# Scattered additions in pairs, a finer reload of x, and a reordered begin of the first attention in a six-layer kernel

## The chip, the cores and the metric

The kernel runs on one core of a Trainium2 chip. The metric is the device time of one execution in microseconds (us). A core has a matrix engine (PE, with its weight loads PEld), a vector engine (DVE), a scalar engine (ACT), a general engine (POOL), and SP, which here only issues transfers. Each engine works through its own instruction list in order; transfers run beside them on 16 DMA engines. In the profile a line such as L526 is that line of the kernel's file, and "q" behind an engine's name (SPq, POOLq) is its sequencer.

## What is computed

Six residual layers work on `x`, 4096 rows of 256 floats: an expert layer, an attention, the same expert layer again, then a second kind of expert layer, a second attention, and that expert layer again. The change touches the first three and the begin of the fourth. Cut to what matters:

```python
def _L0_ffn_ref(x, Wg, W1, b1, W2, b2):      # E = 8 experts, each takes k = 1024 of the 4096 rows
    S = jax.nn.sigmoid(xt @ Wg).T
    G, I = jax.lax.top_k(S, k)               # an expert's own k rows are all different
    ex = xt[I]
    hid = gelu(einsum('ekh,ehf->ekf', ex, W1) + b1)
    out = (einsum('ekf,efh->ekh', hid, W2) + b2) * G[..., None]
    return zeros_like(xt).at[I.reshape(-1)].add(out.reshape(-1, h))

x = x + 0.5 * _L0_ffn_ref(_layernorm(x), ...)
x = x + _L0_attn_ref(_layernorm(x), ...)     # q, k, v each rotated (rope), 16 heads of 16, causal
x = x + 0.5 * _L0_ffn_ref(_layernorm(x), ...)
x = x + 0.5 * _L1_ffn_ref(_layernorm(x), ...)
x = x + _L1_attn_ref(_layernorm(x), ...)
x = x + 0.5 * _L1_ffn_ref(_layernorm(x), ...)
```

## The kernel before

`x` lies on the chip as 32 tiles of 128 rows; four tiles are one sequence (a "group", QT = 4). PE, DVE, ACT and POOL run in program order in the layers of interest (`manual_schedule`); SP's order is chosen by a scheduler from what is ready.

**Expert layer (`_ffn0`, L246).** It runs twice (n = 0 and 1). A gate (`Gate`, L1285) comes first. In layer 0 it is the loop at L276 over eight groups g: for even g the moments of the next two groups (`moments`, L1312: bn_stats L175 and bn_aggr L176 for each tile on DVE, one square root on ACT L181, five small DVE operations L210 to L215), then `columns` (L1336: PE transposes, ACT copies L1343), `rows` of the next group (L1326: normalises four tiles, tiles 1 and 3 on POOL, the others on DVE), `thin` (L1345: scores with `wg`, ACT copy `line` L1353) and `tall` of the group before (L1355: PE transposes the scores, ACT copies them into `raw` at L1362). `sigmoid` (L1364) then clips at -87, takes exp on ACT, adds 1, takes the reciprocal. A search for each expert's 1024th score follows (L321), and `indices` (L430) makes the row lists.

Then come eight experts (L539). For each: `gather` (L471, eight indirect transfers issued by POOL), `turn` (transposes), `hidden` (64 matmuls of 512 columns on each half, PE and ACT), `outputs` (L512). `outputs` makes eight tiles `ob` of 128 rows; each is added into `acc_d` in memory by one indirect transfer with addition (L526), issued by POOL, and each waits until the one before it has landed. In layer 0 `clear` (L149) writes zeros into the buffers of a later layer, two transfers for each expert, issued by SP before `hidden`. After the last expert SP reloads `x` from `acc_d` in four pieces of eight tiles (L558).

**First attention (`_attn0`, L566).** It loads its weights on SP (L578 to L594), POOL writes its constants (L597 to L631), DVE makes `mask_h` and `ident_h` (L610, L612). The begin (L849 to L882) takes the moments of tiles 0 to 7 (`ln_range`, with the square root on ACT), prepares the bias `bo` with a small matmul (L855), then handles sequence 0: `normal` (L641: xn on DVE, and POOL adds `bo` to the residual rows, L653), `turned` (transposes), `rope` (L662) for k, q and v. One rope half copies the product to `raw` (ACT, L671), then POOL makes the cosine and the sine product (L673, L675), and for the second half POOL combines them (L680, L681). `sides` (L697) projects and SP copies the heads into `wide` tiles (L714). The moments of the other tiles stand between. `top` (L739) makes scores on PE and DVE takes the row maxima (L759). From there a loop of 16 pairs of steps runs; the gate of the next expert layer is spread over its last part as `units` (L1371).

**Second kind of expert layer (`ffn1_before`, L1784).** It begins with the moments of tiles 0 to 7 (L1794), `normal` of groups 0 and 1, `columns`, and then logits, a routing and POOL's sends.

`ln_guess` (L184) is a second way to 1/sqrt, with twelve small DVE operations and none on ACT.

Of the kernel before, what the change touches and what calls it, by code (L numbers as in the profile page):

```python
# [9 lines left out]
F32 = mybir.dt.float32  # L10
# [9 lines left out]
P = 128  # L20
# [45 lines left out]
class Kernel:  # L66
    def __init__(self, ctx, tc, w):
# [7 lines left out]
        self.late = self.wide = None  # L75


        self.x = resid.tile([P, TT, D], F32, name="x")
        x_in = w["x"].rearrange("(t p) d -> p t d", p=P)
        for g in range(TT // QT):  # L80
# [68 lines left out]
    def clear(self, zero, part, parts):  # L149

        for t in PARTS:
            rows = self.slots_d[t].rearrange("(j p) d -> p j d", p=P)
            a, b = slot_tiles(t) * part // parts, slot_tiles(t) * (part + 1) // parts
            self.nc.sync.dma_start(out=rows[:, a:b, :], in_=bc(zero, 1, b - a))


    def ln_tiles(self, pool):
# [88 lines left out]
    def _ffn0(self, ctx, n, front):  # L246
# [253 lines left out]
        def hidden(e, h, w1, beside=lambda: None):  # L500
            hid[h] = work.tile([P, FC, CH], F32, name="hid")
            for f in range(FC):
# [6 lines left out]
                nc.scalar.activation(hid[h][:, f, :], hp, AF.Gelu, bias=b1[:, e, f : f + 1])  # L509
                beside()  # L510

        def outputs(e, h, w2, following=None):  # L512
            for i in range(QT):
                if i % 2 == 1 and following is not None:
                    turn(following, i // 2)
                st = h * QT + i
                op = psum.tile([P, D], F32, name="op", tag="o")
                for f in range(FC):
                    nc.tensor.matmul(  # L519
                        op, lhsT=hid[h][:, f, i * P : i * P + P], rhs=w2[:, f, :],  # L520
                        start=(f == 0), stop=(f == FC - 1),
                    )
                ob = work.tile([P, D], F32, name="ob", bufs=4)
                nc.vector.tensor_tensor(ob, op, b2[:, e, :], ALU.add)  # L524
                nc.scalar.mul(ob, ob, gate[:, e, st : st + 1])  # L525
                nc.gpsimd.indirect_dma_start(  # L526
                    out=acc_d[:, :],
                    out_offset=bass.IndirectOffsetOnAxis(ap=idx[:, e, st : st + 1], axis=0),
                    in_=ob, in_offset=None,
                    bounds_check=NT - 1, oob_is_err=True, compute_op=ALU.add,  # L530
                )

        if n == 0:
            zero = pool.tile([P, D], F32, name="zero")
# [4 lines left out]
        for e in range(E0):  # L539
            w1, w2 = wts  # L540
            if e + 1 < E0:
                wts = weights(e + 1)
            coming = indices(e + 1) if e + 1 < E0 else iter(())
            if n == 0:
                self.clear(zero, e, E0)

            hidden(e, 0, w1, lambda: advance(coming, 1))
            advance(coming, 99)
            if e + 1 < E0:
                gather(e + 1)  # L550
            if e == 0:
                turn(0, 1)
            outputs(e, 0, w2)
            hidden(e, 1, w1)
            outputs(e, 1, w2, e + 1 if e + 1 < E0 else None)
        for g in range(4):
            ts = slice(g * 8, g * 8 + 8)
            nc.sync.dma_start(out=self.x[:, ts, :], in_=acc_rows[:, ts, :])  # L558


    def attn0(self, front):
# [4 lines left out]
    def _attn0(self, ctx, front):  # L566
# [43 lines left out]
        nc.vector.tensor_copy(mask_h, maskT)  # L610
        ident_h = pool.tile([P, P], BF16, name="ident_h")
        nc.vector.tensor_copy(ident_h, self.ident)  # L612

        tops = []
        for i in range(4):
# [21 lines left out]
        def bank(shape, name):  # L637
            return psum.tile(shape, F32, name=name, tag="m", bufs=2)


        def normal(b):  # L641
            mv, rstd = stats
            st = seq[b] = {}
            xn = st["xn"] = work.tile([P, QT, D], F32, name="xn", bufs=1)
            st["xnT"] = work.tile([P, DC, CH], F32, name="xnT", bufs=1)
            for i in range(QT):
                t = b * QT + i
                nc.vector.tensor_scalar(
                    xn[:, i, :], self.x[:, t, :], mv[:, t, 0:1], rstd[:, t : t + 1],
                    ALU.subtract, ALU.mult,  # L650
                )
            rows = self.x[:, b * QT : b * QT + QT, :]
            nc.gpsimd.tensor_tensor(rows, rows, bc(bo, 1, QT), ALU.add)  # L653

# [7 lines left out]
        def rope(b, n, c):  # L662
            st = seq[b]
            pp = bank([P, CH], "pp")
            for k in range(DC):
                nc.tensor.matmul(
                    pp, lhsT=first[n][:, k, c * P : c * P + P], rhs=st["xnT"][:, k, :],
                    start=(k == 0), stop=(k == DC - 1),
                )
            raw = work.tile([P, CH], F32, name="raw")  # L670
            nc.scalar.copy(raw, pp)  # L671
            xc = work.tile([P, CH], F32, name=f"xc{c}", bufs=1)
            nc.gpsimd.tensor_tensor(xc, raw, cos, ALU.mult)  # L673
            xs = work.tile([P, CH], F32, name=f"xs{c}", bufs=1)
            nc.gpsimd.tensor_tensor(xs, raw, sin, ALU.mult)  # L675
            st["half", c] = (xc, xs)
            if c == 1:
                r = st["rope", n] = work.tile([P, DC, CH], F32, name=f"rope{n}", bufs=1)
                (ec, es), (oc, os_) = st["half", 0], st["half", 1]
                nc.gpsimd.tensor_tensor(r[:, 0, :], ec, os_, ALU.add)  # L680
                nc.gpsimd.tensor_tensor(r[:, 1, :], oc, es, ALU.subtract)  # L681
# [169 lines left out]
        bvw = work.tile([P, CH], F32, name="xs0", bufs=1)[:, : DC * P].rearrange("p (c o) -> p c o", c=DC)  # L851
# [6 lines left out]
        normal(0)  # L858
        for c in range(DC):
            turned(0, c)  # L860
        for n in (1, 0):
            for c in range(DC):
                rope(0, n, c)
        self.ln_range(pool, stats, 8, 8)
        for c in range(DC):
            rope(0, 2, c)
# [418 lines left out]
class Gate:  # L1285


    def __init__(self, k, n, ctx):
        self.k, nc = k, k.nc
        self.pool = pool = ctx.enter_context(k.tc.tile_pool(name=f"g0_{n}", bufs=1, reuse_waits="tile"))  # L1290
        self.xn_d = k.dram.tile([NT, D + E0], F32, name=f"xn_d{n}")
        self.acc_d = k.dram.tile([NT, D], F32, name=f"acc_d{n}")
        self.xn_rows = self.xn_d.rearrange("(t p) d -> p t d", p=P)
        self.acc_rows = self.acc_d.rearrange("(t p) d -> p t d", p=P)
        self.wg = pool.tile([P, DC, E0], F32, name="wg")
        nc.sync.dma_start(out=self.wg, in_=k.w["Wg"].rearrange("(c p) e -> p c e", p=P))
# [58 lines left out]
    def tall(self, g, bank):  # L1355
        nc = self.k.nc
        tp = bank()[:, : QT * E0]
        for i in range(QT):
            nc.tensor.transpose(
                tp[:, i * E0 : i * E0 + E0], self.line[g][:, i * P : i * P + P], self.k.ident[:E0, :E0]  # L1360
            )
        nc.scalar.copy(self.raw[:, g * QT : g * QT + QT, :].rearrange("p t e -> p (t e)"), tp)  # L1362

    def sigmoid(self, t0, t1):  # L1364
        nc, r = self.k.nc, self.raw[:, t0:t1, :]
        nc.vector.tensor_scalar(r, r, -87.0, None, ALU.max)
# [417 lines left out]
def ffn1_before(k, f):  # L1784
# [3 lines left out]
    with ExitStack() as ctx, k.tc.manual_schedule(engines={E.PE, E.DVE, E.Activation, E.Pool, E.SP}):  # L1788
# [305 lines left out]
```

## Time and profile before

| what | us |
|---|---|
| runs before | 3935.51, 3939.59, 3947.90 (median 3939.59) |
| the profiled execution | 3937.4 |
| its span | 3935.6 |
| PE busy | 3603.7 (92% of the span) |
| DVE / ACT / POOL busy | 1870.9 / 1451.8 / 1206.7 |
| gate, search and first indices of layer 0 | 0 to 98 |
| experts, layer 0: first `hp` to last `op` | 111 to 574 |
| first attention, from the reload to the next gate's end | 582 to 1252 |
| experts, layer 2 | 1308 to 1771 |

In a line of the page's groups or of the timeline stand start and length in us, the engine, the line, the operation, output and inputs by name, shapes, a count, and in brackets how long the engine had been idle and what ended that. PEclk is the clock that PE was granted. The profile shows one execution; the median of the runs is 2.2 us above it.

### The profile page before, as it was taken

How to read it: one execution, taken by the hardware profiler on the slowest of the kernel's cores; microseconds unless marked ns; L12 is line 12 of the kernel's file. 1: busy time of each engine (PE TensorE's matmuls, PEld its weight loads, DVE VectorE, ACT ScalarE, POOL GpSimd, SP SyncE). 2: the span in 40 equal slices, each digit the busy share in tenths (PEclk: the TensorE clock that was granted, in tenths of full speed). 3: DMA queues.
4: the chain of work that ended last, by engine and by line, in shares of the span. 5: the costliest groups of instructions: out<-in, count | busy, mean ns of one | idle time of the engine just before them, and what ended most of it. 6: DMA issues, size and time to landing. Idle time of an engine off the chain costs nothing.

```text
span 3935.6 us, 51751 instructions
## 1 busy us (share of the span) xinstructions
PE 3603.7 (92%) x18250; PEld 2258.1 (57%) x18250; DVE 1870.9 (48%) x4435; ACT 1451.8 (37%) x2936; POOL 1206.7 (31%) x1072
## 2 busy tenths in 40 slices
PE   4999987999996799996899999999999999989978
PEld 1566653555553466664588745555555554568855
DVE  7221216555554312206534566666555576554444
ACT  3222222444444222221133355555555554523311
POOL 2333334343331333332553312220000005404364
PEclk7999997999988899997999999999999999989989
DMA  9433321100113233324367401000000001146643
GB/s 323 135 77 71 72 45 56 25 19 23 28 33 93 55 70 72 74 30 145 102 217 229 138 20 30 28 22 1 1 1 1 1 1 59 49 122 221 181 146 105
DMA packets 256268, 306.97 MB, mean 78 GB/s; under 512 B 34448, under 2 KB 226064, under 8 KB 255760
## 3 DMA queue, kind: packets, MB, share of 16 engines
q1 hardware_dynamic: 206864, 202.43, 16.4%
q0 software_dynamic: 49152, 101.24, 10.9%
q8 instruction: 151, 2.47, 0.3%
q14 instruction: 101, 0.83, 0.1%
HBM read 161.48 MB, written 133.69 MB: 75 GB/s over the span
## 4 chain that ended last, share of the span: by engine, by line
PE 76%; issue 6%; DVE 6%; DMA 5%; POOL 4%; ACT 3%; POOLq 0%; SPq 0%; DVEq 0%; ACTq 0%
PE hp L505 10%; PE op L519 10%; PE sp L1051 6%; PE tp L1071 6%; PE zp L1098 6%; PE pq L1029 6%; PE hs L1713 4%; PE yp L1113 3%; PE pv L1018 3%; PE yps L1735 2%; PE st L795 2%; PE z L809 2%; PE hp L1640 2%; POOL slots_d L1426 2%; PE sp L750 2%
## 5 line engine op out<-in xcount | busy, mean ns | idle before, releaser
L505 PE MATMUL hp<-exT,w 128*128 128x512 f32 x1024 | 456.0, 599 | 0.0
L519 PE MATMUL op<-w,hid 128*128 128x256 f32 x2048 | 451.9, 379 | 0.0
L1060 ACT ACTIVATE ex<-sp,nmax 128x512 f32<-128x512 f32 x512 | 344.7, 685 | 242.2 <-DVE nmax L1057 242.2
L1533 POOL DMA_INDIRECT yg<-ys_d,slot x256 | 267.1, 1044 | 513.2 <-DVE x L1546 296.5
L519 PEld LDWEIGHTS op<-w,hid 128*128 128x128 f32 x2048 | 387.0, 190 | 63.9 <-issue 14.3
L524 DVE TENSOR_TENSOR ob<-op,b 128x256 f32<-128x256 f32 x128 | 54.3, 424 | 642.9 <-PE op L519 567.5
L526 POOL DMA_INDIRECT acc_d<-ob,idx x128 | 210.8, 1646 | 442.4 <-ACT ob L525 204.5
L1057 DVE TENSOR_REDUCE nmax<-sp 128x2 f32<-128x1024 f32 x256 | 301.5, 1219 | 80.4 <-PE sp L1051 80.2
L759 DVE CUSTOM_DVE_ANT_0 junk<-sp,mask 128x128 bf16<-128x128 f32 (+3 forms) x512 | 251.0, 490 | 183.9 <-PE sp L750 159.7
L505 PEld LDWEIGHTS hp<-exT,w 128*128 128x128 f32 x1024 | 193.9, 192 | 222.3 <-issue 217.6
L1071 PEld LDWEIGHTS tp<-ident,ex 128*128 128x128 f32 x2048 | 234.3, 141 | 146.8 <-issue 85.2
L1713 PE MATMUL hs<-w_sb,xT 128*128 x1264 | 308.7, 388 | 2.3 <-DMA xs<-slots_d 1.3
L509 ACT ACTIVATE hid<-hp,b 128x512 f32<-128x512 f32 x256 | 175.9, 687 | 323.9 <-PE hp L505 323.9
L1071 PE MATMUL tp<-ident,ex 128*128 128x128 f32 x2048 | 272.4, 275 | 6.7 <-ACT ex L1060 5.4
L1713 PEld LDWEIGHTS hs<-w_sb,xT 128*128 128x128 f32 x1264 | 247.2, 196 | 38.8 <-ACT xT L235 2.6
L1426 POOL DMA_INDIRECT slots_d<-wide,slot x176 | 174.4, 991 | 307.1 <-DVE past L1519 144.1
L1051 PE MATMUL sp<-qk,qk 64*128 64x512 f32 x1024 | 254.4, 615 | 0.0
L1029 PE MATMUL pq<-xnT,wide 128*128 128x512 f32 x512 | 245.8, 603 | 1.2 <-ACT xnT L235 0.8
L237 DVE COPY eT<-tp 128x512 f32<-128x512 f32 x256 | 176.8, 691 | 138.9 <-PE tp L1071 138.1
L235 ACT COPY eT<-tp 128x512 f32<-128x512 f32 x256 | 149.6, 585 | 240.2 <-PE tp L1071 240.2
L1098 PE MATMUL zp<-eT,v 128*64 128x512 f32 x1024 | 235.6, 602 | 0.0
L525 ACT ACTIVATE ob<-ob,gate 128x256 f32<-128x256 f32 x128 | 65.0, 508 | 413.9 <-DVE ob L524 413.9
(342 smaller groups left out, 5472.5 us busy)
## 6 DMA issues: line engine op xcount, KB each, us to landing
xs<-slots_d SPq DMA_DIRECT2D x156, 256.0 KB, 2.9
ys_d<-ys SPq DMA_DIRECT2D x156, 256.0 KB, 2.6
w<-in_W SPq DMA_DIRECT2D x32, 1024.0 KB, 6.1
w_sb<-in_w SPq DMA_DIRECT2D x24, 512.0 KB, 7.7
slots_d<-zero SPq DMA_DIRECT2D x7, 1536.0 KB, 13.2
xn_d<-xn SPq DMA_DIRECT2D x16, 512.0 KB, 3.1
acc_d<-x SPq DMA_DIRECT2D x16, 512.0 KB, 4.3
x<-acc_d SPq DMA_DIRECT2D x8, 1024.0 KB, 9.7
```

Of the source, the lines that this page charges most:

```text
L505: nc.tensor.matmul(hp, lhsT=w1[:, c, f * P : f * P + P], rhs=exT[e][:, c, h * CH : h * CH + CH], start=(c == 0), stop=(c == DC - 1),)
L519: nc.tensor.matmul(op, lhsT=hid[h][:, f, i * P : i * P + P], rhs=w2[:, f, :], start=(f == 0), stop=(f == FC - 1),)
L759: nc.vector.tensor_tensor_reduce(out=junk[:, :wd], in0=sps[h // 2][:, h % 2, at : at + wd], in1=mask[:, S - wd :], scale=1.0, scalar=NEG, ...
L1029: nc.tensor.matmul(pp, lhsT=(wq, wk)[a][:, k, c * P : c * P + P], rhs=xnT[b][:, k, :], start=(k == 0), stop=(k == DC - 1),)
L1051: nc.tensor.matmul(sp[:, j, :], lhsT=q[r, qt * P : qt * P + P], rhs=k[r, :], start=True, stop=True)
L1057: nc.vector.tensor_reduce(nmax, sp, AX.X, ALU.max, negate=True)
L1060: nc.scalar.activation(ex[:, j, :], sp[:, j, :], AF.Exp, bias=nmax[:, j : j + 1], accum_out=ch["sums"][:, qt, j : j + 1],)
L1071: nc.tensor.transpose(tp[:, k, :], ch["ex", qt][:, j, k * P : k * P + P], self.ident)
L1098: nc.tensor.matmul(zp[DK1 * j : DK1 * j + DK1, :], lhsT=v[b, h][:, k, at : at + DK1], rhs=ch["eT"][:, j, k, :], start=(k == 0), stop=(k == ...
L1426: inst = nc.gpsimd.indirect_dma_start(out=self.slots_d[h][:, :], out_offset=bass.IndirectOffsetOnAxis(ap=self.slot[h][:, r, t : t + 1], ax ...
L1533: inst = nc.gpsimd.indirect_dma_start(out=y[:, r, :], out_offset=None, in_=self.ys_d[h][:, :], in_offset=bass.IndirectOffsetOnAxis(ap=self ...
L1713: nc.tensor.matmul(hp[:, u].rearrange("p a i -> p (a i)"), lhsT=st[j]["xT"][:, u, c, :], rhs=self.w13[:, bass.ds(st[j]["e"][u], 1), c, :]. ...
```

## The change

- `wg` is loaded once, as the first transfer of the kernel, and both gates use it.
- `clear` is issued by ACT and stands behind the first `hidden` of its expert.
- The addition becomes `scatter`: within an expert it waits for the second last addition before it; the first one of an expert waits for the last two.
- The reload of `x` has eight pieces of four tiles, which wait for the last two additions.
- In the first attention, ACT makes `mask_h` and `ident_h`. For sequence 0 the sine product is made by DVE from the matmul's own output, and the residual's bias is added by `offset`, later. The begin takes moments four tiles at a time with `ln_guess`, and its order is new.
- `tall` copies with DVE and clips there; `sigmoid` has no clip any more.
- `ffn1_before` takes moments of four tiles with `ln_guess` before each of its first two `normal`.

```diff
+        self.wg = const.tile([P, DC, E0], F32, name="wg")
+        nc.sync.dma_start(out=self.wg, in_=w["Wg"].rearrange("(c p) e -> p c e", p=P))
...
-            self.nc.sync.dma_start(out=rows[:, a:b, :], in_=bc(zero, 1, b - a))
+            self.nc.scalar.dma_start(out=rows[:, a:b, :], in_=bc(zero, 1, b - a))
...
+        def scatter(e, st, ob):
...
+            before = added[-2:] if st == 0 else added[-2:-1]
+            for other in before:
+                tc.add_manual_dep(inst, other.name, SYNC, reason="an expert's own rows are all different")
+            key = f"acc{n}{e}"
+            tc.declare_no_dep(inst, group=key, keep=before, reason="an expert's own rows are all different")
...
+            hidden(e, 0, w1, lambda: advance(coming, 1))
             if n == 0:
                 self.clear(zero, e, E0)
-
-            hidden(e, 0, w1, lambda: advance(coming, 1))
...
-        for g in range(4):
-            ts = slice(g * 8, g * 8 + 8)
-            nc.sync.dma_start(out=self.x[:, ts, :], in_=acc_rows[:, ts, :])
+        for g in range(TT // QT):
+            ts = slice(g * QT, g * QT + QT)
+            inst = nc.sync.dma_start(out=self.x[:, ts, :], in_=acc_rows[:, ts, :]).ins
+            for other in added[-2:]:
+                tc.add_manual_dep(inst, other.name, SYNC, reason="all additions are there")
...
-        nc.vector.tensor_copy(mask_h, maskT)
+        nc.scalar.copy(mask_h, maskT)
...
-            nc.gpsimd.tensor_tensor(xs, raw, sin, ALU.mult)
+            if b == 0:
+                nc.vector.tensor_tensor(xs, pp, sin, ALU.mult)
+            else:
+                nc.gpsimd.tensor_tensor(xs, raw, sin, ALU.mult)
...
-        self.ln_range(pool, stats, 0, 8)
+        def moments(b, n):
+            for t in range(b * QT, b * QT + n * QT):
+                self.ln_mean(pool, stats, t)
+            self.ln_guess(pool, stats, b * QT, n * QT)
+
+        moments(0, 1)
+        normal(0)
+        for c in range(DC):
+            turned(0, c)
         nc.vector.tensor_scalar(bqk[:, 0, :], bqk[:, 0, :], 1.0 / HD0**0.5, None, ALU.mult)
+        for n in (1, 0):
+            for c in range(DC):
+                rope(0, n, c)
...
+        for a in (1, 0):
+            sides(0, 0, a)
+        for c in range(DC):
+            rope(0, 2, c)
...
         nc.vector.tensor_tensor(bo, bo, bp, ALU.add)
...
+        offset(0)
+        moments(1, 1)
         normal(1)
         for c in range(DC):
             turned(1, c)
-        for a in (1, 0):
-            sides(0, 0, a)
-        self.ln_range(pool, stats, 16, 8)
-        self.ln_range(pool, stats, 24, 8)
+        moments(2, 3)
+        moments(5, 3)
...
-        nc.scalar.copy(self.raw[:, g * QT : g * QT + QT, :].rearrange("p t e -> p (t e)"), tp)
+        nc.vector.tensor_scalar(
+            self.raw[:, g * QT : g * QT + QT, :].rearrange("p t e -> p (t e)"), tp, -87.0, None, ALU.max
+        )
...
-        nc.vector.tensor_scalar(r, r, -87.0, None, ALU.max)
...
-        k.ln_range(f.route, f.stats, 0, 8)
-        f.normal(0)
-        f.normal(1)
+        for g in range(2):
+            for t in range(g * QT, g * QT + QT):
+                k.ln_mean(f.route, f.stats, t)
+            k.ln_guess(f.route, f.stats, g * QT, QT)
+            f.normal(g)
```

More of the change, by code (lines that the diff above doesn't have):

```diff
@@ L510, in hidden @@
                 beside()
+        added = []
+        def scatter(e, st, ob):
+            inst = nc.gpsimd.indirect_dma_start(
+                out=acc_d[:, :],
+                out_offset=bass.IndirectOffsetOnAxis(ap=idx[:, e, st : st + 1], axis=0),
+                in_=ob, in_offset=None,
+                bounds_check=NT - 1, oob_is_err=True, compute_op=ALU.add,
+            ).ins
+            before = added[-2:] if st == 0 else added[-2:-1]
[3 more added lines that the diff above has]
+            tc.declare_no_dep(inst, group=key, keep=before, reason="an expert's own rows are all different")
+            tc.add_to_no_dep_group(key, inst)
+            added.append(inst)
         def outputs(e, h, w2, following=None):
@@ L525, in outputs @@
                 nc.scalar.mul(ob, ob, gate[:, e, st : st + 1])
[L526 to L531, printed above, removed]
+                scatter(e, st, ob)
         if n == 0:
@@ L609, in _attn0 @@
         mask_h = pool.tile([P, P], BF16, name="mask_h")
-        nc.vector.tensor_copy(mask_h, maskT)
+        nc.scalar.copy(mask_h, maskT)
         ident_h = pool.tile([P, P], BF16, name="ident_h")
-        nc.vector.tensor_copy(ident_h, self.ident)
+        nc.scalar.copy(ident_h, self.ident)
         tops = []
@@ L651, in normal, with offset @@
                 )
+            if b > 0:
+                offset(b)
+        def offset(b):
             rows = self.x[:, b * QT : b * QT + QT, :]
@@ L847, in unit @@
                     units.pop(0)(strip)
-        self.ln_range(pool, stats, 0, 8)
+        def moments(b, n):
[6 more added lines that the diff above has]
+            turned(0, c)
         nc.vector.tensor_scalar(bqk[:, 0, :], bqk[:, 0, :], 1.0 / HD0**0.5, None, ALU.mult)
-        bvw = work.tile([P, CH], F32, name="xs0", bufs=1)[:, : DC * P].rearrange("p (c o) -> p c o", c=DC)
+        for n in (1, 0):
+            for c in range(DC):
+                rope(0, n, c)
+        bvw = work.tile([P, CH], F32, name="zs", bufs=1)[:, : DC * P].rearrange("p (c o) -> p c o", c=DC)
         nc.vector.tensor_copy(bvw, bc(bv, 2, P))
+        for a in (1, 0):
+            sides(0, 0, a)
+        for c in range(DC):
+            rope(0, 2, c)
         bp = bank([P, D], "bp")
@@ L856, in _attn0 @@
         nc.vector.tensor_tensor(bo, bo, bp, ALU.add)
[L858 to L866, printed above, removed]
+        offset(0)
+        moments(1, 1)
         normal(1)
@@ L1294, in __init__ @@
         self.acc_rows = self.acc_d.rearrange("(t p) d -> p t d", p=P)
-        self.wg = pool.tile([P, DC, E0], F32, name="wg")
-        nc.sync.dma_start(out=self.wg, in_=k.w["Wg"].rearrange("(c p) e -> p c e", p=P))
+        self.wg = k.wg
         self.raw = pool.tile([P, TT, E0], F32, name="raw")
```

## Prediction

> **What bounds the kernel now.** I read the page's chain and its slices first, then the timeline of the four places that the diff touches, and last the windows at the reload of x.
>
> ```profile
> PE 76%; issue 6%; DVE 6%; DMA 5%; POOL 4%; ACT 3%; POOLq 0%; SPq 0%; DVEq 0%; ACTq 0%
> ...
> PE   4999987999996799996899999999999999989978
> ```
>
> The chain of waits is PE's for three quarters, and no group in the change's experts or attention waits long inside its stage. PE falls below 8 in slices 1, 7, 13, 14 and 19 and near the end: the seams between layers. So only a seam can pay: the gate of layer 0, its first gather, the step into the first attention, and the step into the fourth layer.
>
> ```profile
> 22.83 0.17 ACT L1362 COPY raw<-tp 128x32 f32<-128x32 f32 x1
> 22.91 0.20 ACT L181 ACTIVATE y<-y 128x8 f32<-128x8 f32 x1
> 42.78 2.37 DVE L1366 TENSOR_SCALAR raw<-raw 128x192 f32<-128x192 f32 x1 [1.76 <-ACT raw L1362]
> 46.07 3.57 PE L1349 MATMUL tp<-xnT,wg 128*8 128x512 f32 x4 [2.26 <-ACT xnT L1343]
> 98.44 1.22 POOL L476 DMA_INDIRECT ex<-xn_d,idx  x1 [53.41 <-DVE idx L467]
> 110.76 12.36 PE L505 MATMUL hp<-exT,w 128*128 128x512 f32 x24
> 1307.59 12.97 PE L505 MATMUL hp<-exT,w 128*128 128x512 f32 x24
> 578.01 1.55 POOL L526 DMA_INDIRECT acc_d<-ob,idx  x1 [3.00 <-DMA acc_d<-ob,idx]
> 581.85 5.45 SPq L558 DMA_DIRECT2D x<-acc_d  x4
> 583.46 11.01 DVE L610 CAST mask_h<-raw 128x128 bf16<-128x128 f32 x1 [9.38 <-POOL raw L605]
> 590.84 3.55 POOL L631 MEMSET value<- 128x2048 f32 x2
> 608.82 5.63 PE L666 MATMUL pp<-xnT,wkT_sb 128*128 128x512 f32 x8
> 619.64 1.19 DVE L213 SCALAR_TENSOR_TENSOR u<-mv,u 128x8 f32<-128x8 f32 x1
> 644.48 0.69 DVE L759 CUSTOM_DVE_ANT_0 junk<-sp,mask 128x512 bf16<-128x512 f32 x1
> 651.04 0.56 DVE L759 CUSTOM_DVE_ANT_0 junk<-sp,mask 128x384 bf16<-128x384 f32 x1 [3.56 <-PE sp L750]
> 1784.98 0.43 DVE L175 BATCH_NORM_STATS2 bn<-x 128x6 f32<-128x256 f32 x1 [13.45 <-DMA x<-acc_d]
> 1791.69 3.94 PE L1611 MATMUL tp<-ident,wide 128*128 128x128 f32 x16 [20.67 <-DVE wide L1417]
> ```
>
> The reader should see four things. In the gate the copy of `tall` (22.83) stands just ahead of the square root on ACT. The first `hp` of layer 0 comes 12.3 us after its first gather (98.44 to 110.76). The reload starts at 581.85, two additions after the last `ob`, and `rope` at 608.82. And the CAST of 11.01 us on DVE, a copy of 128 columns, lasts as long as POOL's run of MEMSETs beside it: some DVE operations stand still while POOL runs.
>
> **1. Gate of layer 0.** `tall` moves from ACT to DVE, in program order behind the `xn` tiles and ahead of the next bn_stats. PE ends `tall(0)` at 22.66, while DVE started the next moments at 16.85. So eight tiles of statistics, 8 x 0.53 = 4.2 us, now follow 22.66 plus a copy of 0.2, and the square root goes from 22.91 to about 27.4: +4.5. At the second pair of groups the same wait costs +3.6 (the pair's statistics less the room that was there), at the last group, with four tiles, +1.8: 9.9 together. Against it, the maximum at 42.78 (2.37 us, beside POOL's MEMSETs) leaves the path: -2.3. One `thin` after a longer idle PE would run as the cold ones (3.57 at 46.07) and not as the short ones (1.88): +1.5. The early `wg` saves PE's first wait of 3.1 us, but x's first piece lands one transfer later and DVE starts later; I take 0, as groups 0 and 1 are then held by the statistics. Sum +9.1; low end +6 if half of the statistics find room, high +11 with a second cold `thin`.
>
> **2. Zeros behind the first `hidden`, on ACT.** In layer 2, without zeros, the same step from gather to `hp` took 1299.3 to 1307.59, 8.3 us, against 12.3. I take all of the difference, -4.0 (-2 if half of it is weights). Each issue takes 0.5 to 3.6 us (L154, median 3.55), so ACT is held up to 7.1 us for an expert. What hides it: the next GELU is due some 14 us later, behind the turn and the first outputs, and four `ob` buffers. Without that cover it would be 8 x up to 7 us; PE is saturated inside an expert's 57.8 us, and I take 0. SP loses two issues per expert, and its weights are not late now.
>
> The Trainium skill speaks against a gain here: in "DMA: Bandwidth & Descriptors", section "Issuing engines are not separate DMA queues", moving issues to another engine saves issue time only, as all share the 16 DMA engines. By that rule the step gives 0 by itself and the whole sum would be 4.0 higher; the two rows (12.3 and 8.3) say that what counts is when the zeros travel, so I stay with them.
>
> **3. Additions in pairs.** The spacing of one after the other at the tail is 4.5 us; `ob` comes every 3.45. The last `ob` is ready at 574.6, so the last issue follows at about 574.9 and lands after the median 3.8, at 578.7, against 581.85: -3.1 in each expert layer, for whatever uses it in steps 4 and 6. POOL's count of issues is unchanged (1.55 each). In the middle experts nothing changes: PE sets their pace.
>
> **4. Begin of the first attention.** Eight pieces of 512 KB: the first lands 4.1 to 4.3 us after its issue (the 512 KB loads of x have a minimum of 4.1), at 583. Its four tiles take 2.1 us of statistics, at 585. But POOL's constants, which end at 590.84 + 3.55 = 594.4 and began at 582.02 behind the last addition, move only by the 3.1: 578.9 to 591.3, and the first small operation of `ln_guess` meets them as the CAST did. So I put the end of the guess (12 operations, 2.35 us at L184's later use) at 593.6. Four `xn` and the turn give `rope` at 596.2, against 608.82: -12.6. The floor is 594, when `wkT` is there: 4.19 MB of x and weights at the 359 GB/s of the windows after 580.4, plus a copy.
>
> Then the lead meets DVE's queue. k's rope is done 10.2 us after the start and q's 15.2 (8 POOL operations of 1.27 in place of 12, and DVE's four sine products of 0.69, whose operand is in PSUM; the row L772, of that kind, never took over 0.69). Then v to +20.8, `bp` and `bo` to +22, `moments(1,1)` to 24.3, its guess beside the last POOL operations (two held, 1.19 as at 619.64) to 29.7, `xn(1)` to 31.1, and then 24 tiles x 0.53 plus 2 guesses x 2.4 = 17.6, all ahead of the first row maximum on DVE: 596.2 + 31.1 + 17.6 = 644.9, against 644.48. Before, statistics of these tiles filled DVE's waits between ropes; now they stand in one block. So the start of the loop is unchanged; PE has its first scores ready earlier and the hole of 3.56 us at 651.04 closes, though after an idle PE the matmuls are longer: I take -1.5. Low end -8, when the statistics fit beside the ropes' waits; high +5, when more of the guess is held.
>
> A second rule bears here. The Trainium skill, "SBUF — State Buffer", section "Who interferes with whom", says that the loser of the port the two engines share is blocked for the other's whole instruction. By it the guess would wait out one MEMSET, not the run of them, `rope` would start at 594, and the sum would be 2.2 lower at the most; the row of 11.01 us says the run, and it decides.
>
> ACT's `mask_h` and `ident_h` (0.2 each) wait for POOL's constant with nothing due behind them before the first `xnT` copies. POOL's `offset(0)` (2.35) moves behind `rope` v; the next `offset` follows it as before.
>
> **5. Gate of layer 2,** in the attention: 8 copies of 0.2 on DVE and one maximum less, on an engine busy 48%, but a bank is held until DVE comes to it: +0.3 (-0.5 to +3).
>
> **6. Into the fourth layer.** x's first piece is there at 1780.3 (-3.1, and -1.5 for the smaller piece) against 1784.98, so the first `xn` comes 6 us earlier (four tiles, a guess, no table for the root). But DVE then does two rounds of statistics, guess and `xn`, and the logits of the third group are ready at 1797.0 against 1798.7: -1.7 (-4.5 to 0).
>
> **Sum.** 9.1 - 4.0 + 0 - 1.5 + 0.3 - 1.7 = +2.2 against the profiled 3937.4: 3939.6. The median of the runs is 2.2 above the profile: 3941.8, say 3942. Low ends: 6 - 4 - 8 - 0.5 - 4.5 = -11, high ends: 11 - 2 + 5 + 3 + 0 = +17.
>
> **Rivals.** A, faster: the leads survive. DVE takes the 24 tiles between the ropes' products, as PE's matmuls and POOL's products leave it waiting, and the fourth layer keeps 4.7. Then 9.1 - 4.0 - 12.6 + 0.3 - 4.7 = -11.9: 3928. For it: DVE was idle for 9.38 us ahead of the CAST and is light in the ropes. Against: program order; the blocks stand behind `offset(0)` in the text.
>
> B, slower: in the attention's begin the guess of group 1 and its `xn` meet POOL's queue one operation at a time, as 619.64 shows (1.19 for an operation of 0.2). If nine of POOL's twelve products (1.27) and the `offset` (2.35) are still queued, less the two counted (2.4): +11.4, so +13.6: 3953. It decides from the third held operation on. For it: the row; and DVE's sine products now feed POOL's queue. Against: by 616 only the last combinations and `offset(0)` should be left.
>
> C, the change at the gate doesn't do what step 1 says: DVE's copies find room and only the maximum's saving is left, -2.3 in place of +9.1: -9.2, 3930. For it: DVE is 48% busy. Against: 22.66 is PE's end, and the order is fixed.
>
> **Chances.** The forecast 0.55, A 0.18, B 0.18, C 0.09. 0.3% is 11.8 us (3927.8 to 3951.4), about what a measurement of this kernel tells from no change. The forecast's own range, 3933 to 3950, is within it almost wholly (0.51, 0.01 below, 0.03 above); A is split 0.11 below and 0.07 within, B 0.15 above and 0.03 within, C 0.03 below and 0.06 within. So faster 0.15, same 0.67, slower 0.18. The range, 3928 to 3957, goes from the low ends' sum (which is where A lies) to the high ends'; B is inside, and a tenth is left out on each side.
>
> **What would show it.** Step 1: in the gate DVE's L175 starts after PE's `tall`, near 22.9, and the search's first copy, at 52.31 before, near 60. Step 2: 8.3 us from gather to `hp`, and no PE gap beside ACT's issues. Step 3: the last additions 3.45 apart. Step 4: `rope` near 596 and the first row maximum near 645, both shifted by the 5 us of steps 1 and 2; if the maximum comes 10 earlier it is A, 10 later B. Step 6: first transposes 6 us earlier, the third group's only 1.7. The forecast is wrong if an expert's 57.8 us grow: ACT's issues would then cost eight times what they delay.

## The result, and the profile after

| | median of the runs, us | ratio to the kernel before (95% interval) |
|---|---|---|
| before | 3942.82 (20 runs) | 1 |
| changed | 3947.98 (20 runs) | 1.0015 (1.0008 to 1.0021) |

The changed kernel is slower by 0.15%, some 5 us (3 to 8 by the interval). Its profiled execution has a span of 3944.0 against 3935.6. Of the twelve runs below, those of experiments 1 and 3 and the first of experiments 4 and 5 were taken on a chip on which the kernel before took 3944.83, the other eight on two chips on which it took 3995.83 and 3997.17 with a wider scatter; from those eight mainly distances within the trace are used. Some runs there are over 1.5% longer than the fastest of their kernel; the ratios leave them out, and of the two profiles that fell on such runs (e9_oldbegin, e11_three) nothing is read behind the fourth layer's begin.

The page of the changed kernel, its chain and its slices of PE:

```profile
PE 42%; issue 5%; DVE 4%; POOL 3%; DMA 3%; ACT 1%; POOLq 0%; DVEq 0%; SPq 0%; ACTq 0%
...
PE   4899986999996799996899999999999999989978
```

The shares of the chain add to 58%: it was followed back only part of the way, so its 42% is not to be set against the 76% of before. PE's busy time is the same (3605.9 against 3603.7): what changed is the seams. They are in the timeline (start, length, engine, line, operation; in brackets the idle time before and what ended it). First the gate of layer 0 and the first gather:

```profile
21.85 0.41 PE L1386 MATMUL tp<-ident,line 8*128 8x8 f32 x4
22.30 0.19 DVE L1389 TENSOR_SCALAR raw<-tp 128x32 f32<-128x32 f32 x1 [4.73 <-PE tp L1386]
26.97 0.21 ACT L184 ACTIVATE y<-y 128x8 f32<-128x8 f32 x1 [4.44 <-DVE y L183]
27.70 3.58 PE L1376 MATMUL tp<-xnT,wg 128*8 128x512 f32 x4 [4.07 <-ACT xnT L1370]
...
108.84 1.22 POOL L479 DMA_INDIRECT ex<-xn_d,idx  x1 [49.63 <-DVE idx L470]
...
117.20 12.35 PE L508 MATMUL hp<-exT,w 128*128 128x512 f32 x24
```

DVE stood idle for 4.73 us until PE had transposed the scores (22.30), and only then took the eight tiles' statistics; the root follows at 26.97 and not at 22.91. PE waits 4.07 us at 27.70 and its matmuls are then the long ones (3.58 in place of 1.88). The first gather is 10.4 us late, and the gather to `hp` takes 8.36 us in place of 12.32.

The begin of the first attention:

```profile
581.34 1.55 POOL L518 DMA_INDIRECT acc_d<-ob,idx  x1 [1.90 <-ACT ob L545]
585.25 6.99 SPq L572 DMA_DIRECT2D x<-acc_d  x8
589.15 0.52 POOL L641 MEMSET widek<- 128x512 f32 x1
589.36 0.43 DVE L178 BATCH_NORM_STATS2 bn<-x 128x6 f32<-128x256 f32 x1 [8.83 <-DMA x<-acc_d]
591.62 6.24 DVE L195 TENSOR_SCALAR v<-mv 128x4 f32<-128x4 f32 x1
594.29 3.55 POOL L647 MEMSET value<- 128x2048 f32 x2
602.70 5.07 PE L686 MATMUL pp<-xnT,wkT_sb 128*128 128x512 f32 x8
626.26 2.34 POOL L673 TENSOR_TENSOR x<-x,bo_sb 128x1024 f32<-128x1024 f32 x1
626.36 2.26 DVE L197 TENSOR_SCALAR i<-v 128x4 int32<-128x4 int32 x1
649.60 0.68 DVE L782 CUSTOM_DVE_ANT_0 junk<-sp,mask 128x512 bf16<-128x512 f32 x1
```

The last addition waits for its `ob` alone. The first operation of the guess, 0.2 us of work, lasts 6.24: it ends at 597.86, when POOL's writes end (594.29 + 3.55 = 597.84). Not every DVE operation is held there: the statistics of the four tiles run beside the same MEMSETs from 589.36 on in their usual 0.39 to 0.43 us each. `rope` starts 6.1 us earlier than before on the clock, and 12.6 earlier after the 6.4 that the experts started late; yet the first row maximum comes at 649.60, 5.1 later than before. As a mark for the loop's steady part I take the eleventh of its subtractions (`qm`, L795): 841.10, and 833.96 before. And into the fourth layer:

```profile
1784.56 0.43 DVE L178 BATCH_NORM_STATS2 bn<-x 128x6 f32<-128x256 f32 x1 [8.45 <-DMA x<-acc_d]
1790.06 2.15 PE L1639 MATMUL tp<-ident,wide 128*128 128x128 f32 x8 [14.47 <-DVE wide L1445]
1795.94 2.21 PE L1639 MATMUL tp<-ident,wide 128*128 128x128 f32 x8 [3.73 <-DVE wide L1445]
1801.21 1.95 PE L1639 MATMUL tp<-ident,wide 128*128 128x128 f32 x8
```

The first transposes come 1.6 us before those of the old kernel, the third group's 2.5 us after.

### The profile page after: what moved, and what is told of

It is laid out like the page before. It is cut to its first block, busy times and chain, and to the rows that moved or that the text cites. A ratio compares the mean times of both kernels' runs of the same rounds, so it can differ in the third digit from the quotient of the medians.

```text
span 3944.0 us, 51792 instructions
## 1 busy us (share of the span) xinstructions
PE 3605.9 (91%) x18250; PEld 2256.5 (57%) x18250; DVE 1872.7 (47%) x4493; ACT 1448.4 (37%) x2916; POOL 1188.8 (30%) x1066
## 3 DMA queue, kind: packets, MB, share of 16 engines
q0 software_dynamic: 49152, 101.24, 10.4%
## 4 chain that ended last, share of the span: by engine, by line
PE 42%; issue 5%; DVE 4%; POOL 3%; DMA 3%; ACT 1%; POOLq 0%; DVEq 0%; SPq 0%; ACTq 0%
PE sp L1079 6%; PE tp L1099 6%; PE zp L1126 6%; PE pq L1057 6%; PE hs L1741 4%; PE yp L1141 3%; PE pv L1046 3%; PE yps L1763 2%; PE hp L1668 2%; POOL slots_d L1454 2%; DMA yg<-ys_d,slot 2%; PE tpx L1727 1%; POOL yg L1561 1%; PE rp L1113 1%; PE lg L1647 1%
## 5 line engine op out<-in xcount | busy, mean ns | idle before, releaser
L518 POOL DMA_INDIRECT acc_d<-ob,idx x128 | 201.6, 1575 | 419.0 <-ACT ob L545 366.8
L479 POOL DMA_INDIRECT ex<-xn_d,idx x128 | 131.4, 1026 | 298.2 <-DVE idx L470 252.5
```

## The experiments

Every kernel is the changed one with one edit, if nothing else is said. Times of events are from each run's own trace.

**1. The copy of tall on ACT again.**

```diff
-        nc.vector.tensor_scalar(
-            self.raw[:, g * QT : g * QT + QT, :].rearrange("p t e -> p (t e)"), tp, -87.0, None, ALU.max
-        )
+        nc.scalar.copy(self.raw[:, g * QT : g * QT + QT, :].rearrange("p t e -> p (t e)"), tp)
...
     def sigmoid(self, t0, t1):
+        nc.vector.tensor_scalar(r, r, -87.0, None, ALU.max)
```

> The changed kernel with tall's copy on ACT again and the clip back in sigmoid; the rest as changed. My theory (step 1: DVE's copy waits for PE and holds the next groups' statistics) expects the first gather near 98.4 in place of 108.84, so 9 to 10.5 us less than the changed kernel, some 4 to 6 us below the kernel before. The rival (the gate is late because x's first piece and wg share the start of the transfers) expects the copy to matter little: the first gather stays above 106, and the time is within 3 us of the changed kernel.

Ratio to before 0.9957 (0.9944 to 0.997), -17 us. The timeline of this kernel:

```profile
22.34 0.17 ACT L1389 COPY raw<-tp 128x32 f32<-128x32 f32 x1
22.42 0.20 ACT L184 ACTIVATE y<-y 128x8 f32<-128x8 f32 x1
...
97.94 1.22 POOL L479 DMA_INDIRECT ex<-xn_d,idx  x1 [53.43 <-DVE idx L470]
```

The root is at 22.42 and the gather at 97.94, as my theory said; the rival falls. The time fell by more than the 4 to 6 us below before that I expected. Against the changed kernel the profiled execution is 15.8 us shorter: 10.9 at the first gather, 2.8 between the loop's steady part and layer 2's first `hp`, 5.3 behind the last routing's maximum, in code that the edit doesn't touch, less 3.2 lost between. So the trace gives the gate its 10.9 us; for the rest I have no cause.

**2. Tall on DVE, behind the next statistics.** Run twice, on two chips.

```diff
+                if g % 2 == 0 and g > 0:
+                    front.tall(g - 2, bank)
                 front.thin(g, bank)
-                if g > 0:
+                if g % 2 == 0 and g > 0:
                     front.tall(g - 1, bank)
...
+            front.tall(6, bank)
             front.tall(7, bank)
```

> The changed kernel with tall's copy still on DVE and clipped there, but two tall at a time and behind the statistics of the next pair of groups. My theory (the cost of step 1 is the place in DVE's order, not the engine) expects the first gather between 95 and 99, like with the copy on ACT (97.9) less the maximum's 2.3, and so 10 to 14 us less than the changed kernel. The rival (a copy on DVE holds the PSUM bank and PE wherever it stands) expects the first gather above 103.

> The changed kernel with tall behind the next statistics, once more, beside the others of this set. My theory expects the first gather near 97.7 again and 10 to 14 us less than the changed kernel, so 5 to 9 us below the kernel before. On the granted clock: most runs with the new begin showed it at 0.88, 0.78 and then 0.84 in the stretches 20 to 40 and 60 to 80 us after the first row maximum, the last run of this kernel showed 1.00; if the begin's long PE idle makes it, the dip is there this time.

The first gather came at 97.67 and 97.48; the line of the first run:

```profile
97.67 1.22 POOL L482 DMA_INDIRECT ex<-xn_d,idx  x1 [50.08 <-DVE idx L473]
```

So the place in DVE's list costs the 10 us, not the engine. The whole: 1.0011 (0.9988 to 1.0035) in the first set, where the runs lay between 3986.7 and 4037.9 and nothing follows from the ratio, and 0.9958 (0.9939 to 0.9977) in the second. On the clock see experiment 7.

**3. Additions one after the other.**

```diff
-            before = added[-2:] if st == 0 else added[-2:-1]
+            before = added[-1:]
```

> The changed kernel with every addition waiting for the one before it again. My theory (step 3) expects the reload 3.0 us later in both expert layers, and since the lead lies on the path in both places, the next stage later by as much: +6 us in all against the changed kernel. The rival (the lead is off the path, DVE or the weights set the next stage) expects +0 to +2 us, with the reload later and the first rope and the first logits unmoved.

Ratio 1.0035 (1.0022 to 1.0048) against 1.0015: +8 us. From the first `hp` to the reload 471.7 us in place of 468.1 in layer 0, and 470.2 in place of 467.1 in layer 2; from the reload to `rope` 17.4 and 17.5, and to the routing's first maximum in the fourth layer 29.0 in both kernels. The 3.6 and 3.1 us pass on whole, so the rival falls. The trace had a surprise ahead of all this, in code that the edit does not touch (scores of groups 3, 6 and 7 in the gate, this kernel first, then the changed one):

```profile
34.53 3.19 PE L1376 MATMUL tp<-xnT,wg 128*8 128x512 f32 x4
54.82 3.28 PE L1376 MATMUL tp<-xnT,wg 128*8 128x512 f32 x4 [1.96 <-ACT xnT L1370]
60.93 3.47 PE L1376 MATMUL tp<-xnT,wg 128*8 128x512 f32 x4 [1.11 <-ACT xnT L1370]
```

```profile
33.99 2.61 PE L1376 MATMUL tp<-xnT,wg 128*8 128x512 f32 x4
53.48 1.88 PE L1376 MATMUL tp<-xnT,wg 128*8 128x512 f32 x4 [1.95 <-ACT xnT L1370]
58.20 1.88 PE L1376 MATMUL tp<-xnT,wg 128*8 128x512 f32 x4 [0.45 <-ACT xnT L1370]
```

After nearly the same idle (1.96 and 1.95 us) the same four matmuls took 3.28 or 1.88. With the blocked gate the first gather stood at 108.14, 108.84, 109.27, 110.61, 111.94, 112.23 and 112.85 in the seven profiles that have it, 110.6 in the mean; with the repaired gate the six profiles lie between 96.5 and 98.9.

**4. The zeros: when, and by whom.** First on SP ahead of the first `hidden`, as before:

```diff
-            self.nc.scalar.dma_start(out=rows[:, a:b, :], in_=bc(zero, 1, b - a))
+            self.nc.sync.dma_start(out=rows[:, a:b, :], in_=bc(zero, 1, b - a))
...
+            if n == 0:
+                self.clear(zero, e, E0)
             hidden(e, 0, w1, lambda: advance(coming, 1))
-            if n == 0:
-                self.clear(zero, e, E0)
```

> The changed kernel with the zeros issued by SP and ahead of the first hidden again. My theory (step 2) expects 12.3 us from the first gather to the first hp in place of 8.4, so +4 us against the changed kernel and no other change. The rival (the engine that issues makes no difference and the gather is slow for the weights) expects the step to stay at 8.4 us and the time within 1 us.

Gather to `hp` 12.32 us (112.23 to 124.55) in place of 8.36: as expected, and the time 1.002 (1.0012 to 1.0029), +2 us against the changed kernel within overlapping intervals. Then only the engine, with the call left behind the first `hidden`:

> The changed kernel with the zeros behind the first hidden as now, but issued by SP. My theory (what counts is when the zeros travel) expects 8.4 us from the first gather to the first hp and the time within 2 us of the changed kernel. The rival (taking the issues off SP is the gain) expects 12.3 us and +4 us.

12.19 us (109.27 to 121.46), and a ratio of 1.0029 (1.0017 to 1.0041), 5 to 6 us above the changed kernel's: by its own words my expectation failed, and both numbers are nearer to the rival's. The row of the zeros' issues, of this kernel and then of the changed one (count; least, median and longest issue in ns; first and last start):

```profile
L157 SPq DMA_DIRECT2D slots_d<-zero x16: 359/3508/5687, 59.7 to 111.5; - x16
```

```profile
L157 ACTq DMA_DIRECT2D slots_d<-zero x16: 366/479/595, 134.1 to 539.1; - x16
```

SP's order is not that of the text: it issued all 16 as soon as they were free to go, 59.7 to 111.5, over the first gather, wherever the call stands (60.0 to 111.9 with the call ahead of `hidden`). On ACT, whose list is in program order, they go out from 134 on, two for each expert. Each also takes 0.48 us to issue in place of 3.5, so the rival, SP's time to issue, has to be told from the time of the transfers. PE's first transpose of gathered rows does that (before, this kernel, the changed one):

```profile
105.70 0.48 PE L492 MATMUL tp<-ident,ex 128*128 128x128 f32 x1 [8.02 <-DMA ex<-xn_d,idx]
116.59 0.48 PE L495 MATMUL tp<-ident,ex 128*128 128x128 f32 x1 [8.09 <-DMA ex<-xn_d,idx]
111.89 0.48 PE L495 MATMUL tp<-ident,ex 128*128 128x128 f32 x1 [3.82 <-DMA ex<-xn_d,idx]
```

It starts 7.26, 7.32 and 3.05 us after the gather's first issue, which is POOL's, and each time it waits for the gathered rows and not for anything that SP loads. So the gather's own transfers were slow while the zeros travelled, and it counts when they travel. That moving them to ACT is what makes their place in the text count is argued from ACT's program order; no kernel here issues them on ACT from the old place.

**5. The statistics out of the attention's begin.**

```diff
-        moments(2, 3)
-        moments(5, 3)
...
+            if p == 0:
+                for i in range(6):
+                    put(i // 2 + 1, i % 2, means, 2 * QT + 2 * i)
+                put(4, 0, guess, 2, 3)
+            if p == 2:
+                for i in range(6):
+                    put(i // 2 + 1, i % 2, means, 5 * QT + 2 * i)
+                put(4, 0, guess, 5, 3)
```

> The changed kernel with the statistics of groups 2 to 7 taken out of the attention's begin and put, two tiles at a time, into the first and the third pair of the loop. My theory (step 4: the lead of rope is lost because 24 tiles of statistics and two guesses, 17.6 us, stand on DVE ahead of the first row maximum) expects the first row maximum near 636 in place of 649.6 and 8 to 13 us less than the changed kernel. The rival (scores come late anyway, from POOL's ropes and the transfers into the wide tiles, or the loop has no room on DVE) expects under 3 us.

```profile
634.83 0.69 DVE L782 CUSTOM_DVE_ANT_0 junk<-sp,mask 128x512 bf16<-128x512 f32 x1 [3.46 <-PE sp L773]
```

The first row maximum came at 634.83, 14.1 us earlier once the gate's 0.7 is taken off, so the block of statistics was what held it. By the ninth of the loop's subtractions (L795 there) 7.2 us were left of it. The ratio was 0.999 (0.9981 to 1.0), -10 us against the changed kernel. Where the other half went:

```profile
688.42 1.26 DVE L195 TENSOR_SCALAR v<-mv 128x12 f32<-128x12 f32 x1
689.73 1.28 POOL L703 TENSOR_TENSOR rope<-xc,xs 128x512 f32<-128x512 f32 x1
689.92 1.12 DVE L198 TENSOR_SCALAR i<-i 128x12 int32<-128x12 int32 x1
690.97 1.26 POOL L704 TENSOR_TENSOR rope<-xc,xs 128x512 f32<-128x512 f32 x1
691.08 1.18 DVE L202 TENSOR_TENSOR u<-i 128x12 f32<-128x12 f32 x1
...
695.40 0.37 PE L807 MATMUL st<-mask_h,ident_h 128*128 128x128 bf16 x2 [5.02 <-DVE top L782]
```

Three operations of 0.17 us ended each with one of POOL's, and PE then stood for 5.02 us. So the guesses were cut into four parts and moved to the second and fourth pair (the four closures hold the lines of `ln_guess` unchanged):

```diff
+            if p in (0, 2):
+                for i in range(6):
+                    put(i // 2 + 1, i % 2, means, (2 if p == 0 else 5) * QT + 2 * i)
+            if p in (1, 3):
+                parts = guesses(2 if p == 1 else 5, 3)
+                for (i, s), run in zip(((0, 0), (0, 0), (0, 1), (1, 0)), parts):
+                    put(i, s, run)
```

> The changed kernel with the statistics of groups 2 to 7 in the first and third pair of the loop, as in the run before, but with the two guesses cut into four parts that stand in the second and fourth pair, where POOL makes no ropes. In the run before, the guess at 688.4 took 5.4 us beside POOL's ropes and PE then waited 5.0 us for a row maximum; that run kept 7 of 14 us. My theory (the held small operations cost the other half) expects 9 to 13 us less than the changed kernel and the loop's steady part 10 to 14 us earlier. The rival (DVE's room in the first pairs is too small for the 24 tiles themselves) expects the same 6 to 7 us.

The loop's steady part came 12.3 us earlier than in the changed kernel once the experts' start (119.04 against 117.20) is taken off, and at the place of the 5.02 PE waited 1.63 us:

```profile
695.23 0.27 PE L807 MATMUL st<-mask_h,ident_h 128*128 128x128 bf16 x2 [1.63 <-DVE top L782]
```

So the held operations were the other half. The ratio of that set, 1.0015 (0.9984 to 1.0047), is too wide to say more.

**6. The fourth layer's begin as before.**

```diff
-        for g in range(2):
-            for t in range(g * QT, g * QT + QT):
-                k.ln_mean(f.route, f.stats, t)
-            k.ln_guess(f.route, f.stats, g * QT, QT)
-            f.normal(g)
+        k.ln_range(f.route, f.stats, 0, 8)
+        f.normal(0)
+        f.normal(1)
```

> The changed kernel with the begin of the fourth layer as before: moments of tiles 0 to 7 in one go with the square root on ACT, then both normal. My theory (step 6: two rounds of statistics, guess and xn stand one after the other on DVE) expects the logits of the third group 2 to 3.5 us earlier after the reload than the 20.4 us of the changed kernel, and 2 to 3.5 us less in all. The rival (the transfers of the eight pieces set it) expects 20 us after the reload again and the time within 1 us.

From the reload to the third group's transposes 19.15 us in place of 20.42, and to the routing's maximum 27.8 in place of 29.0: 1.2 won, less than the 2 to 3.5. The first logits waited 1.18 us for the transfer of `gw` there and took 3.60 us; in the two later kernels with the same edit they took 1.96 and the maximum came 25.6 and 25.4 us after the reload, 3.4 less than in the changed kernel. The ratio (1.0081, 1.0051 to 1.0111) speaks against the edit; in the profiled execution the added time lies behind this layer, in the same code, between the maximum at 1812.7 and the last layer's at 3557.9 (1745 us, where the changed kernel took 1696 on the first chip). The three other profiles of that chip took 1735 to 1774 us there without the edit. I take the trace for the step, and the whole as not shown.

**7. The begin of the attention as before,** on top of experiment 2 (mask casts on DVE, POOL's sine product, `offset` inside `normal`, the old order with the roots on ACT):

```diff
-        moments(0, 1)
+        self.ln_range(pool, stats, 0, 8)
...
         for n in (1, 0):
             for c in range(DC):
                 rope(0, n, c)
...
+        self.ln_range(pool, stats, 8, 8)
...
-        moments(2, 3)
-        moments(5, 3)
+        self.ln_range(pool, stats, 16, 8)
+        self.ln_range(pool, stats, 24, 8)
```

> The changed kernel with tall behind the next statistics, and with the begin of the first attention as in the kernel before (constants' casts on DVE, POOL's sine product, offset inside normal, the old order with the roots on ACT); additions, reload and fourth layer as changed. It is to be compared with the next run, which has the new begin. My theory (step 4: the new begin wins 12.6 us for rope and loses them to the block of statistics) expects the two within 3 us of each other, rope some 26 us after the reload in place of 17.5, and the first row maximum 62 to 64 us after it in both. The rival (the new begin is worth its lead) expects 8 us or more between them.

After the reload `rope` came at 25.8 us and the first row maximum at 61.4 (17.5 and 64.8 with the new begin, beside it in the same set); the steady part at 255.0 and 256.4. So the lead of 8 us is gone by the maximum, as expected, and the old begin is even 3.3 us ahead there. The times, 0.999 (0.9962 to 1.0017) against 0.9958 (0.9939 to 0.9977), lie some 13 us apart in favour of the new begin, which is what the rival put, with intervals that overlap. In the traces the kernel with the old begin still leads by 1.9 us at the fourth layer's routing (1798.2 against 1800.1), and the code behind it is the same; where the 13 us arise, and whether they are real, stays open. As to the clock, the windows of 10 us that begin 20, 30 and 60 us after the first row maximum, in the two runs of experiment 2 (the third number from the end is the granted clock):

```profile
657.40:667.40 10.00, 7.91 (x66) 4.34 (x65) 6.54 (x25) 5.06 (x6) 9.36 (x8) 1.00 0.00 2
667.40:677.40 10.00, 10.00 (x65) 5.11 (x64) 4.58 (x19) 5.05 (x7) 3.07 (x3) 1.00 0.02 6
...
697.40:707.40 10.00, 9.56 (x108) 5.66 (x101) 8.11 (x37) 4.09 (x6) 2.76 (x2) 1.00 0.12 28
```

```profile
659.30:669.30 10.00, 7.91 (x55) 4.12 (x57) 6.89 (x25) 4.40 (x5) 9.30 (x9) 0.90 0.01 2
669.30:679.30 10.00, 10.00 (x66) 6.14 (x59) 3.46 (x16) 3.76 (x5) 2.37 (x3) 0.76 0.01 2
...
699.30:709.30 10.00, 9.57 (x93) 4.62 (x92) 5.64 (x25) 3.34 (x5) 1.60 (x1) 0.84 0.11 26
```

The same kernel ran with and without the dip, and the steady part came 250.6 or 256.4 us after the reload. Of these 5.8 us 0.7 were there at the first row maximum, so the dip goes with some 5 us. It isn't made by this begin: the old one has it too, 0.68 from 664.3 to 674.3 us. What makes it stays open.

**8. The parts together:** tall behind the statistics, the cut guesses in the loop, the fourth layer's begin as before; then also POOL's writes of the value tiles behind k's and q's ropes:

```diff
             t = pool.tile([P, QT, H0, 32], F32, name=f"value{i}")
-            nc.gpsimd.memset(t, 1.0)
...
+        for t in values:
+            nc.gpsimd.memset(t, 1.0)
         for c in range(DC):
             rope(0, 2, c)
```

> The changed kernel with tall behind the next statistics, the statistics of groups 2 to 7 and their cut guesses in the loop, and the fourth layer's begin as before. My theory adds the parts: 11.2 (gate) + 11.8 (spread) + 1.3 (fourth layer) = 24 us less than the changed kernel, 17 to 22 us below the kernel before. The rival (the gains use the same room, or the clock takes them back) expects under 15 us less than the changed kernel.

> As the run before, and POOL's writes of the two value tiles (3.55 us) stand behind k's and q's ropes. My theory (POOL's run of writes holds the first guess until 594.3 + 3.55) expects the held operation to be 3.5 us shorter (2.7 in place of 6.24), rope 2.5 to 3.5 us earlier after the reload than 17.5 and as much less time. The rival (the weights' transfer sets rope) expects rope at 17 us or more after the reload and no difference.

Three parts: 0.9963 (0.9935 to 0.9991), 15 us below the kernel before where 17 to 22 were expected, with the routing's maximum of the fourth layer at 1779.5 in place of 1809.8. Four parts: 0.9933 (0.9911 to 0.9955), 27 us below the kernel before, the lowest ratio of this study and below that of the changed kernel. The held operation in the last:

```profile
579.78 2.74 DVE L195 TENSOR_SCALAR v<-mv 128x4 f32<-128x4 f32 x1
581.96 0.53 POOL L644 MEMSET widek<- 128x512 f32 x1
588.49 6.53 PE L688 MATMUL pp<-xnT,wkT_sb 128*128 128x512 f32 x8 [0.99 <-DMA wkT_sb<-in_wkT]
```

It ends at 582.52 with the last write (581.96 + 0.53). `rope` came 15.1 us after the reload, 2.4 earlier where 2.5 to 3.5 were expected, as it then waited for `wkT`: the weights are the next floor, where the prediction had put it (594, 15.3 us after the last addition's landing at 578.7). The loop kept nothing of these 2.4 us (the steady part 1.3 us later after the reload than with three parts, in a stretch with the clock at 0.86 and 0.67), and the difference between 0.9963 and 0.9933 is not shown to come from this edit.

## Why the prediction was right, point by point

The measured column is the profiled execution; each row is what a stage added.

| step | predicted, us | measured, us |
|---|---|---|
| 1 gate, to the first gather | +9.1 | +10.4 (+12.1 in the mean of seven profiles) |
| 2 gather to `hp` | -4.0 | -4.0 |
| 3 and 4, `hp` to the loop's steady part (eleventh subtraction) | -1.5 | +0.7 |
| 5 to layer 2's first `hp` | +0.3 | -1.0 |
| 6 to the routing's maximum in the fourth layer | -1.7 | -3.6 |
| sum there | +2.2 | +2.5 |
| layers that the change doesn't touch | 0 | +5.9 |

**Right in mechanism and size.** Step 1 was right in how it comes about (22.30, 26.97), and experiments 1 and 2 took it away. Step 2's difference between the two rows was the price; its reason, the place in the text, needs an engine that keeps the order of the text, which SP did not. The Trainium skill ("DMA: Bandwidth & Descriptors", section "Issuing engines are not separate DMA queues") lets a change of engine save issue time only. That does not speak against the 8.36, which came with the time of the transfers. Step 3's 3.1 was 3.0. Step 4 put `rope` 12.6 us earlier and it was 12.6; the maximum was put 0.4 us later than before, apart from the gate's shift, and came 1.3 earlier. No expert grew: from the first `hp` to the reload it is 3.0 us less, as the additions alone give.

**Mis-sized.** Step 1's "One `thin` after a longer idle PE would run as the cold ones: +1.5" should have been two or more and a spread: in this execution three groups were longer (3.58, 2.61 and 3.52 in place of 1.88) and the old long one was short (1.88 at 58.20 in place of 3.57), +2.4 in all, and in the seven profiles the same gate lay between +9.7 and +14.4. The mean's 3 us over +9.1 would take the forecast of +2.2 to +5.2, the difference of the medians. That it fits so well is partly luck, as the misses of the other rows, +2.2, -1.3 and -1.9 us, add up to -1.0 only. Step 4's "I take -1.5" lies between the +0.7 of this execution and the -5.3 of experiment 2's first run (from `hp` to the steady part, 717.9 against 723.2), and most of what lies between them goes with the clock's dip (experiment 7). Step 6 won more than I said, of it 1.4 ahead of the reload: layer 2's experts took 4.5 us less where 3.1 was expected. From the reload on, the new begin cost 0.9 us where 1.4 was expected.

**The last row** is no step of the change. The same code took 433.0, 433.0, 432.9, 435.0, 436.7 and 438.3 us from the last routing's maximum to the end in the profiles of before, experiment 1, the first of 5, the first of 4, 3 and the changed kernel: the profiled pair overstates the difference, and the medians' 5.2 us stand.

**The rivals.** A, that the leads survive, did not come; experiment 5 shows what the lead in the attention would have needed, the statistics out of the way. B, that more of the guess meets POOL, did not come either: two operations were held (0.65 and 2.26 us), as was counted. C fell with the 10.4 us. The Trainium skill ("SBUF — State Buffer", section "Who interferes with whom") has the loser of the shared port wait for the other's whole instruction. Read as one operation for one, that fits beside POOL's products (1.26, 1.12, 1.18 us above) and not beside a run of MEMSETs: 6.24 and 2.74 us, to the end of the run each time.

## What to carry to other kernels

An operation that saves time by itself may cost more by where it stands: on an engine in program order it makes all behind it wait for what it waits for, so before a copy is moved to another engine, look up what stands behind it there. A lead at the begin of a stage is worth what the next engine's queue lets through; here 12.6 us went into 17.6 us of statistics (632.0 to 649.6) that could be done later. And a call's place in the text counts only on an engine that keeps that order.

## What the runs showed of the hardware that was not expected

Two groups of four small matmuls with nearly the same idle time before them (1.95 and 1.96 us) took 1.88 or 3.28 us, in two executions of the same code, and such groups spread the gate by up to 4.7 us. A DVE TENSOR_SCALAR beside back-to-back MEMSETs of POOL got in only behind the last of them (6.24 and 2.74 us), while BATCH_NORM_STATS2 beside the same MEMSETs kept its 0.43 us, and beside POOL's products a small operation got in after one (1.12 to 1.26 us). And the granted clock dipped to 0.76 for 10 us, some 30 us into the loop, in one run of a kernel and not in another.
